# Products that nobody reads, in TensorE's pauses between the sums of a graph attention layer

## The chip, the cores and the metric

The kernel runs on one core of a Trainium2 chip. A core has several engines, each with an instruction stream of its own that it works through in order: TensorE (PE in the profile; its loads of the stationary operand are shown apart, as PEld), VectorE (DVE), ScalarE (ACT), GpSimd (POOL, which here issues the gathers) and SyncE (SP). Engines wait for each other through semaphores; data lie in SBUF, the accumulators of TensorE in PSUM, the inputs and large intermediates in HBM. The metric is the time of one execution in microseconds on the device, less is better.

## The reference

A graph of N = 6250 nodes and E = 100000 edges, width D = 512, H = 8 heads of DK = 64. Edges come sorted by `src`, which is the node that receives. Cut to what matters:

```python
def gnn(x, src, dst, att_bias):                    # x is already normalised
    q, k, v = [(x @ W + b).reshape(n, H, DK) for W, b in ((Wq, bq), (Wk, bk), (Wv, bv))]
    logits = einsum('ehd,ehd->eh', q[src] / sqrt(DK), k[dst]) + att_bias
    p = exp(logits - segment_max(logits, src)[src])
    att = p / segment_sum(p, src)[src]
    y = segment_sum(att[:, :, None] * v[dst], src)
    return y.reshape(n, H * DK) @ Wo + bo

x = x + gnn(layernorm(x), src, dst, edge_attr_8)
x = x + ffn(layernorm(x))
```

The `ffn` is a small network on 160 columns: it decodes two 4-bit numbers per operand and two flags from each row, runs three layers of 160 x 160 with relu between them, and adds a few one-hot values to the row. Everything is float32.

## The kernel before

**Before the main loop (0 to about 640 us).** Keys of the nodes are sorted, so that nodes of like degree are handled together, and TensorE makes k and v for all nodes (L467). They are written to a table in HBM, `kv_d`, with one row of 1024 floats (k, then v) for each node.

**The main loop (about 640 to 3200 us).** The nodes are taken in 49 blocks of 128, one node to a partition. A block has as many slots as its largest degree asks for (`CAP`, 804 slots in all); a slot holds one edge for each of its 128 nodes. A block's slots are split into parts of at most 12, 91 parts in all, and a part is worked on in pairs of slots, 425 pairs in all, each in a buffer `kvt` of shape [128, 2, 1024] from a pool of 11.

For each pair:

- POOL gathers its rows of `kv_d` with one indirect DMA for each slot (L110, `kv<-kv_d,rec`), and somewhat ahead the records of the edges (L110, `rec<-rec_d,eid`).
- `pump()` advances work of other blocks by one step: the next block's projection (`project`: transposes L803, ACT's copy `xT` L805, q from L809 and L810), the end of an earlier part (`part_end`: L1064 and L1068 add its sum p_y to y, L1072 copies a first one), an earlier block's output (`attend_out`: transposes L833 and L834, ACT's copies L836 and L838, the output projection L842 and L843) and steps of the small network (`alu`: L892, L906, L919, L926, L933).
- `dots()`: DVE multiplies the k half by the node's q, in place (L814), and sums by head (L815) into `dot`. After this the k half of the buffer holds products that nothing in the kernel reads again.

At the end of a part, `softmax()` turns `dot` into weights: DVE L744 to L751, ACT's exponential L752, and ACT's copy of the weights into PSUM (L756), into one of the two halves of the tile `pp`, turn by turn. What comes next in a part, `sums()`, is put off until the first pair of the next part has had its `dots()`: the denominator (L767), then for each pair `weigh()` multiplies the v half by the weights, on DVE with the weights read from `pp` (L825), on ACT with a scalar for each head for the last one or two whole pairs (L823), and TensorE adds the slots up into `p_y` by products with the identity matrix (L1105, 1608 passes in all, two for each slot since float32 takes two).

**What sets the order.** The program is written under a manual schedule: each engine does its instructions in the order in which the program issues them. Waits are put in from the tiles that an instruction reads and writes. The tiles of the main loop come from pools with `reuse_waits="tile"`, so a buffer is free again when the last reader of the tile that it held is done. A gather into a `kvt` buffer so waits for the L1105 passes that read it. `pp` is one tile for the whole loop, `tr` has one buffer in PSUM, `q`, `p_y` and `mm` two each.

After the loop the last blocks' outputs and the small network are finished (3200 us to the end).

Of the kernel before, what the change touches and what calls it, by code (L numbers as in the profile page):

```python
# [10 lines left out]
F32 = mybir.dt.float32  # L11
# [9 lines left out]
P = 128  # L21
# [22 lines left out]
def gnn_ffn_kernel(  # L44
# [3 lines left out]
    nc = tc.nc  # L48
    N, D = x.shape
    E = src.shape[0]  # L50
    H = edge_attr.shape[1]
# [22 lines left out]
    def ctile(shape, name, dt=F32, pool=const):  # L74
        return pool.tile(shape, dt, tag=name, name=name)
# [33 lines left out]
    def gather(dst_t, table, idx):  # L109
        nc.gpsimd.indirect_dma_start(  # L110
            out=dst_t, out_offset=None, in_=table,
            in_offset=bass.IndirectOffsetOnAxis(ap=idx, axis=0))
# [4 lines left out]
    wq = ctile([P, KC, D], "wq", pool=ow)  # L117
# [105 lines left out]
    def fetch_keys(b):  # L223
        C = CAP[ORDER[b]]
        t, nbuf = ("0", 1) if b == 0 else ("", LA + 3)
        kg = pre.tile([P, C + 1], F32, tag="kg" + t, name="kg", bufs=nbuf)
        gather(kg, words, pos_i[:, ORDER[b]:ORDER[b] + 1])
        st[b] = dict(kg=kg)

    def read_keys(b):  # L230
        C = CAP[ORDER[b]]
        t, nbuf = ("0", 1) if b == 0 else ("", LA + 3)
        f0 = pre.tile([P, 1], F32, tag="f0", name="f0", bufs=2)
        eid = decode(st[b]["kg"], 1, C, f0, t, nbuf, ids=nid[:, b:b + 1])
        rec = pre.tile([P, C, ROW], F32, tag="rec" + t, name="rec", bufs=min(nbuf, LA + 2))
        st[b].update(rec=rec, eid=eid)
# [10 lines left out]
    def fetch_recs(n, last):  # L247

        while fetched[0] < n and fetched[1] is not None and fetched[1][0] <= last:
            b, s = fetched[1]  # L250
            gather(st[b]["rec"][:, s, :], rec_d, st[b]["eid"][:, s:s + 1])
            fetched[:] = fetched[0] + 1, next(wanted, None)
# [481 lines left out]
    ops = ctx.enter_context(tc.tile_pool(name="ops", bufs=2, space=PSUM, **main))  # L734

    turn_ = [0, 0]
    assert CG * H <= P
    pp = ops.tile([P, 2 * P], F32, tag="pp", name="pp", bufs=1)

    def softmax(lg, rec, m0):  # L740


        n = lg.shape[1]
        nc.vector.scalar_tensor_tensor(lg, lg, SCALE, rec[:, :, 1:], op0=OP.mult, op1=OP.add)  # L744
        m = ap_.tile([P, H], F32, tag="m", name="m", bufs=4)
        nc.vector.tensor_reduce(m, lg.rearrange("p c h -> p h c"), AX.X, OP.max)
        if m0 is None:
            nc.vector.tensor_scalar(m, m, FLOOR, None, op0=OP.max)
        else:
            nc.vector.tensor_tensor(m, m, m0, op=OP.max)  # L750
        nc.vector.tensor_tensor(lg, lg, m[:, None, :].to_broadcast([P, n, H]), op=OP.subtract)  # L751
        nc.scalar.activation(lg, lg, AF.Exp)  # L752
        turn_[1] ^= 1
        p_ps = pp[:, turn_[1] * P:turn_[1] * P + n * H].rearrange(
            "p (c h) -> p c h", h=H)
        nc.scalar.copy(p_ps, lg)  # L756
        cor = None
        if m0 is not None:
            cor = ap_.tile([P, H], F32, tag="cor", name="cor", bufs=3)
            nc.vector.tensor_tensor(cor, m0, m, op=OP.subtract)  # L760
            nc.scalar.activation(cor, cor, AF.Exp)
        return m, cor, p_ps
# [36 lines left out]
    def project(xg, s_):  # L799

        pt = ops.tile([P, KC, P], F32, tag="tr", name="tr", bufs=1)
        for c in range(KC):
            nc.tensor.transpose(pt[:, c, :], xg[:, D + c * P:D + (c + 1) * P], ident)  # L803
        xT = o2.tile([P, KC, P], F32, tag="xT", name="xT", bufs=2)
        nc.scalar.copy(xT, pt)  # L805
        yield
        q = s_["q"] = ops.tile([P, D], F32, tag="q", name="q")
        for c in range(KC):
            nc.tensor.matmul(q, xT[:, c, :], wq[:, c, :], start=(c == 0), stop=False)  # L809
        nc.tensor.matmul(q, ones3, bq3, start=False, stop=True)  # L810

    def dots(kvt, n, q, dot, s):
        k = kvt[:, :n, :D]
        nc.vector.tensor_tensor(k, k, q[:, None, :].to_broadcast([P, n, D]), op=OP.mult)  # L814
        nc.vector.tensor_reduce(  # L815
            dot[:, s:s + n, :], k.rearrange("p s (h d) -> p s h d", h=H), AX.X, OP.add)
# [164 lines left out]
    def fetch_nodes(b):  # L981
        if b - 4 in ends:
            run(ends.pop(b - 4))
        xg = ap_.tile([P, 2 * D], F32, tag="xg", name="xg", bufs=4)
        gather(xg, xx_d, nid[:, b:b + 1])
        st[b]["xg"] = xg
# [17 lines left out]
    def pump(kinds="", n=1):  # L1004

        last[1] += 1
        for g in list(going):
            if next(g, True):
                if g in going:
                    going.remove(g)  # L1010
        alu_steps(kinds, n)
        if stores and stores[0][0] + last[0] <= last[1]:
            store()

    def alu_steps(kinds, n):

        while alus and n > 0 and kind[0] in kinds:
            kind[0] = next(alus[0], None)
            if kind[0] is None:
                alus.pop(0)  # L1020
                kind[0] = "P"
            n -= 1

    def run(g):

        while alus and g in alus and g is not alus[0]:
            run(alus[0])
        for _ in g:
            pass
        if g in alus:  # L1030
            kind[0] = "P"
        for l in (going, alus):
            if g in l:
                l.remove(g)
# [78 lines left out]
    for b in range(NB):  # L1113
        C = CAP[ORDER[b]]
        s_ = st[b]
        rec, q = s_["rec"], s_["q"]
        parts = -(-C // PART)
        m = None
        for i in range(parts):
            s0, s1 = C * i // parts, C * (i + 1) // parts  # L1120
            n_ = s1 - s0
            dot = ap_.tile([P, n_, H], F32, tag="dot", name="dot", bufs=2)
            kvs = []
            for s in range(s0, s1, 2):
                n = min(2, s1 - s)
                kvt = kvp.tile([P, 2, 2 * D], F32, tag="kv", name="kv")
                for j in range(n):
                    gather(kvt[:, j, :], kv_d, rec[:, s + j, 0:1].bitcast(I32))
                kvs.append((kvt, n, s - s0))
                done = sum(SLOTS[:b]) + s + n  # L1130
                if done > HOLD:
                    last[0] = 1000
                fetch_recs(FIRST + (TOTAL - FIRST) * done // (TOTAL - LAST), b + LA)
                if s == s0 and i == 0:
                    if b + LA + 2 < NB:
                        fetch_keys(b + LA + 2)
                    if b + 1 < NB:
                        fetch_nodes(b + 1)
                if s == s0 + 2 and i == 0 and b + 1 < NB:
                    pj = project(st[b + 1]["xg"], st[b + 1])  # L1140
                    going.insert(0, pj)


                k = len(kvs) - 1
                pump("" if k < 2 else "D" if s + 2 >= s1 else "DE" if k == 2 else "DEP")
                dots(kvt, n, q, dot, s - s0)
                if s == s0:
                    for f in waiting:
                        f()
                    waiting.clear()  # L1150
                if s == s0 + 2 and i == parts - 1 and b + LA + 2 < NB:
                    read_keys(b + LA + 2)
            m, cor, p_ps = softmax(dot, rec[:, s0:s1], m)
            waiting.append(partial(sums, b, i, parts, dot, cor, p_ps, kvs, n_))
            alu_steps("P", min(4, len(kvs) - 1))
        if b + 1 < NB:
            run(pj)
# [150 lines left out]
```

## Time and profile before

| what | value |
|---|---|
| median of 14 runs | 3280.02 us |
| lowest and highest run | 3246.71 and 3307.73 us |
| time of the profiled execution | 3278.29 us |
| its span, first to last instruction | 3276.4 us |
| mean granted TensorE clock | 0.799 |
| matmul passes / weight loads on PE | 4853 / 4853 |
| instructions on DVE / ACT / POOL | 3502 / 2656 / 1860 |
| moved by DMA | 542.30 MB, mean 166 GB/s |

In the profile, an instruction's line is that of the kernel printed above. A float32 product appears as two passes, a transpose as one. The row `PEclk` gives the clock that was granted to TensorE in each of 40 slices of the span, in tenths. Three groups of the main loop give the scale: 804 gathers of k and v on POOL, each 946 ns with the next one issued some 0.30 us later; 425 products with q on DVE (L814), which take 1.21 us for a whole pair; 425 sums by head (L815), 1.22 us. The copy of the weights into `pp` (L756, 91 times) has a median of 222 ns. In the tables of waits, "issue" is time in which an engine waited for nothing that the profile shows, and "remote" a wait whose releaser the profile doesn't find among the engines of the core.

### The profile page before, as it was taken

What the parts mean: (1) busy time and instruction counts of PE and PEld (TensorE: products, weight loads), DVE (VectorE), ACT (ScalarE), POOL (GpSimd) and SP (SyncE); (2) the same over time, 40 slices, a digit from 0 to 9 for tenths busy, and PEclk for the clock granted to TensorE, in tenths of its full rate; (3) what the DMA queues carried; (4) which work ended last, traced back from release to release, by engine and by line L of the source; (5) the groups of instructions that cost most, each with busy time, mean ns of one, the idle gap of its engine ahead of it and who ended that gap; (6) DMA issues with size and microseconds to landing.
All of it is one profiled execution on the core that took longest, in us unless ns stands there. A gap on an engine that the chain in (4) does not pass through costs nothing.

```text
span 3276.4 us, 20109 instructions
## 1 busy us (share of the span) xinstructions
PE 2055.4 (63%) x4853; PEld 887.1 (27%) x4853; DVE 2007.9 (61%) x3502; ACT 880.8 (27%) x2656; POOL 1709.0 (52%) x1860
## 2 busy tenths in 40 slices
PE   7887218644545646646566676666756738556686
PEld 3443104211212222222222232222322313222233
DVE  9987000176645657655776767767677657766762
ACT  6443004121212112222132222322313213122333
POOL 2011760274666366555656656666566565656530
PEclk9999659866767867877878787887877878878787
DMA  8543103465445356455656556666566554656530
GB/s 277 176 155 107 20 16 133 143 217 193 162 160 186 116 178 200 158 167 173 205 174 197 182 178 200 197 191 188 171 200 201 161 184 159 207 174 211 170 116 17
DMA packets 193964, 542.30 MB, mean 166 GB/s; under 512 B 51831, under 2 KB 53174, under 8 KB 193841
## 3 DMA queue, kind: packets, MB, share of 16 engines
q0 software_dynamic: 154416, 464.27, 44.5%
q1 hardware_dynamic: 39425, 76.67, 6.7%
q8 instruction: 42, 0.69, 0.1%
q14 instruction: 81, 0.66, 0.1%
HBM read 472.60 MB, written 68.22 MB: 165 GB/s over the span
## 4 chain that ended last, share of the span: by engine, by line
PE 37%; another core or an unknown queue 23%; DVE 18%; issue 12%; ACT 6%; POOL 2%; DMA 1%; POOLq 0%; DVEq 0%; SPq 0%; ACTq 0%
PE p_y L1105 12%; PE pm L467 7%; DVE kv L814 4%; PE q L809 4%; PE pm L919 4%; PE pm L842 3%; ACT kv L823 3%; DVE dot L815 3%; DVE kv L825 3%; PE pm L906 2%; PE p L926 2%; DVE key L143 1%; DVE key L144 1%; DMA kv<-kv_d,rec 1%
## 5 line engine op out<-in xcount | busy, mean ns | idle before, releaser
L110 POOL DMA_INDIRECT kv<-kv_d,rec x804 | 760.2, 946 | 765.7 <-PE p_y L1105 298.9
L1105 PE MATMUL p_y<-kv,ident 128*128 128x512 f32 x1608 | 815.3, 663 | 341.5 <-issue 170.0
L110 POOL DMA_INDIRECT rec<-rec_d,eid x804 | 763.8, 950 | 245.2 <-issue 235.4
L814 DVE TENSOR_TENSOR kv<-kv,q 128x1024 f32<-128x1024 f32 (+1 forms) x425 | 490.6, 1154 | 206.6 <-DMA kv<-kv_d,rec 121.8
L1105 PEld LDWEIGHTS p_y<-kv,ident 128*128 128x128 f32 x1608 | 332.4, 212 | 798.2 <-issue 565.1
L815 DVE TENSOR_REDUCE dot<-kv 128x16 f32<-128x1024 f32 (+1 forms) x425 | 494.0, 1162 | 59.3 <-ACT kv L823 22.6
L809 PE MATMUL q<-wq,xT 128*128 128x512 f32 x392 | 226.0, 730 | 363.8 <-issue 190.6
L823 ACT ACTIVATE kv<-kv,dot 128x64 f32<-128x64 f32 x1568 | 387.9, 336 | 40.1 <-issue 40.1
L825 DVE TENSOR_TENSOR kv<-kv,pp 128x1024 f32<-128x1024 f32 (+1 forms) x327 | 352.9, 1139 | 0.0
L842 PE MATMUL pm<-wo,yT 128*128 128x512 f32 x392 | 213.1, 694 | 178.3 <-ACT yT L836 139.4
L805 ACT COPY xT<-tr 128x512 f32<-128x512 f32 x49 | 28.7, 585 | 703.3 <-remote 409.5
L809 PEld LDWEIGHTS q<-wq,xT 128*128 128x128 f32 x392 | 88.1, 236 | 472.9 <-issue 294.7
L467 PE MATMUL pm<-wv,xnT 128*128 128x512 f32 (+1 forms) x392 | 187.9, 614 | 17.3 <-issue 17.1
L467 PE MATMUL pm<-wk,xnT 128*128 128x512 f32 (+1 forms) x392 | 188.5, 622 | 0.0
L842 PEld LDWEIGHTS pm<-wo,yT 128*128 128x128 f32 x392 | 85.3, 226 | 289.1 <-ACT yT L836 145.3
L1068 DVE TENSOR_TENSOR y<-y,p_y 128x512 f32<-128x512 f32 x42 | 28.7, 684 | 205.8 <-remote 141.0
L767 DVE TENSOR_REDUCE den<-dot 128x8 f32<-128x64 f32 (+6 forms) x91 | 24.8, 273 | 198.9 <-ACT dot L752 127.5
L836 ACT COPY yT<-tr 128x512 f32<-128x512 f32 x49 | 28.6, 584 | 438.9 <-remote 246.6
L478 ACT COPY kvt<-pm 128x512 f32<-128x512 f32 (+1 forms) x98 | 57.1, 583 | 317.8 <-remote 132.3
L416 DVE RECIPROCAL rstd<-rstd 128x7 f32<-128x7 f32 (+4 forms) x9 | 1.7, 186 | 211.3 <-ACT rstd L412 159.1
L110 POOL DMA_INDIRECT xg<-xx_d,nid x49 | 46.2, 942 | 148.0 <-DMA kv_d<-kvt 125.7
L433 PE MATMUL tr<-ident,xn 128*128 128x128 f32 (+1 forms) x196 | 31.7, 289 | 135.0 <-ACT xn L424 93.7
(258 smaller groups left out, 2179.5 us busy)
## 6 DMA issues: line engine op xcount, KB each, us to landing
kv_d<-kvt SPq DMA_DIRECT2D x48, 512.0 KB
rec<-rec_d,eid POOLq DMA_INDIRECT x804
kv<-kv_d,rec POOLq DMA_INDIRECT x804
xt<-in_x_dram SPq DMA_DIRECT2D x48, 256.0 KB
xx_d<-xt SPq DMA_DIRECT2D x48, 256.0 KB
xx_d<-xn SPq DMA_DIRECT2D x48, 256.0 KB
rec_d<-R SPq DMA_DIRECT2D x3, 882.0 KB
bt<-in_edge_attr_dram SPq DMA_DIRECT2D x3, 686.0 KB
```

What stands on the lines that cost most here:

```text
L110: nc.gpsimd.indirect_dma_start(out=dst_t, out_offset=None, in_=table, in_offset=bass.IndirectOffsetOnAxis(ap=idx, axis=0))
L467: nc.tensor.matmul(pm[:r], xnT[b][:, c, :r], wkv[nm_][:, c, :], start=(c == 0), stop=(i == 1 and c == KC - 1))
L809: nc.tensor.matmul(q, xT[:, c, :], wq[:, c, :], start=(c == 0), stop=False)
L814: nc.vector.tensor_tensor(k, k, q[:, None, :].to_broadcast([P, n, D]), op=OP.mult)
L815: nc.vector.tensor_reduce(dot[:, s:s + n, :], k.rearrange("p s (h d) -> p s h d", h=H), AX.X, OP.add)
L823: nc.scalar.mul(v[:, i, h], v[:, i, h], p[:, s + i, h:h + 1])
L825: nc.vector.tensor_tensor(v, v, p_ps[:, s:s + n, :, None].to_broadcast([P, n, H, DK]), op=OP.mult)
L842: nc.tensor.matmul(pm, yT[:, c, :], wo[:, c, :], start=(c == 0), stop=False)
L906: nc.tensor.matmul(pm[:, :nt], w0[:, c * P:(c + 1) * P], fT[:, t0:t1], start=True, stop=True)
L919: nc.tensor.matmul(pm[:, :nt], w, h1[:, k, :nt], start=(i == 0), stop=(i == len(terms) - 1))
L926: nc.tensor.matmul(p3[:, :nt], w2[:, c, :], h2[:, c, :nt], start=(c == 0), stop=(c == NC4))
L1105: nc.tensor.matmul(p_y, ident, kvt[:, j, D:], start=(done_ == 0), stop=(done_ == n_ - 1))
```

## The change

The tile `pp` is made twice as wide, and its new half becomes the target of products that nobody reads. In each part, for each pair but the first, after the pair's `dots()` TensorE gets two such products. Each loads 16 columns of the previous pair's k half (after DVE's product with q, hence "one pair behind") as the stationary operand, streams 256 columns of one 128-row block of the query weights `wq`, and writes a [16, 256] result into the new half of `pp`. Nothing else is changed.

```diff
@@ -735,7 +735,8 @@
     turn_ = [0, 0]
     assert CG * H <= P
-    pp = ops.tile([P, 2 * P], F32, tag="pp", name="pp", bufs=1)
+    pp = ops.tile([P, 4 * P], F32, tag="pp", name="pp", bufs=1)
+    idle = pp[:2 * H, 2 * P:]
@@ -1144,6 +1145,12 @@
                 k = len(kvs) - 1
                 pump("" if k < 2 else "D" if s + 2 >= s1 else "DE" if k == 2 else "DEP")
                 dots(kvt, n, q, dot, s - s0)
+
+                if s > s0:
+                    for c in range(2):
+                        nc.tensor.matmul(
+                            idle, kvs[-2][0][:, 0, :2 * H],
+                            wq[:, c, :2 * P], start=True, stop=True)
                 if s == s0:
                     for f in waiting:
                         f()
```

Here `s0` is the first slot of the part, `s` the first slot of the pair, and `kvs` the list of the part's pairs so far, so that `kvs[-2][0]` is the previous pair's buffer.

## The prediction

> **What bounds the kernel now.** I read the page's head first, for the engines and the granted clock, and then the chain that ended last.
>
> ```profile
> PE 2055.4 (63%) x4853; PEld 887.1 (27%) x4853; DVE 2007.9 (61%) x3502; ACT 880.8 (27%) x2656; POOL 1709.0 (52%) x1860
> ...
> PEclk9999659866767867877878787887877878878787
> ...
> PE 37%; another core or an unknown queue 23%; DVE 18%; issue 12%; ACT 6%; POOL 2%; DMA 1%; POOLq 0%; DVEq 0%; SPq 0%; ACTq 0%
> ```
>
> No engine is full. TensorE (PE) carries the largest share of the chain, at a clock granted at 0.6 to 0.8 of full speed through the main loop (640 to 3200 us). There is one core, so "another core" needs an explanation, and the table of waits gives it.
>
> ```profile
> ACT xT L805 <- remote: 409.5, 15, 46.6
> POOL kv L110 <- PE p_y L1105: 298.9, 60, 30.7
> ACT yT L836 <- remote: 246.6, 14, 41.6
> ```
>
> The "remote" waits (us in total, times, longest) are ACT copies of transposes that PE's records show finished long before. PE's signals come late, up to 46.6 us, in 29 episodes on these two lines, 656 us together; the profile does not say why. I call them holds. PE and these waits for PE make 37 + 23 = 60% of the chain. The second row is POOL out of gather buffers, because PE has not summed the old ones. The timeline of one part then shows the place that the change touches, just after such a hold.
>
> ```profile
> 2426.10 0.58 ACT L805 COPY xT<-tr 128x512 f32<-128x512 f32 x1 [33.78 <-remote]
> ...
> 2426.74 5.16 PE L809 MATMUL q<-wq,xT 128*128 128x512 f32 x8 [22.09 <-ACT xT L805]
> 2426.86 0.21 ACT L756 COPY pp<-dot 128x56 f32<-128x56 f32 x1
> ...
> 2427.10 2.95 DVE L825 TENSOR_TENSOR kv<-kv,pp 128x1024 f32<-128x1024 f32 x3
> ...
> 2431.73 0.38 PE L810 MATMUL q<-bq,ones 65*128 65x512 bf16 x1
> ...
> 2431.95 6.17 PE L1105 MATMUL p_y<-kv,ident 128*128 128x512 f32 x14
> ```
>
> Each row has its start and its time. The weights go into the tile pp at 2426.86 while PE still makes q; DVE weighs three pairs under that; PE sums at 2431.95 without a pause. That overlap is what is at stake.
>
> **The change, part by part.** *Products.* 425 pairs in 91 parts give 425 - 91 = 334 places with two products, 668 in all, each of two passes as every f32 matmul here: 1336 passes of 256 columns. Their price comes from rows of that width:
>
> ```profile
> 3218.20 2.33 PE L926 MATMUL p<-h,w 128*8 128x256 f32 x10
> ```
>
> Ten passes take 2.33 us, so one starts every 0.22 us at clock 1.0 (less 0.16 us of tail), twice that at 0.5: 0.86 us a pair warm, 1.71 cold, 288 us or 572 us in all. PE is idle 2560 - 1581 = 979 us of the loop (windows view), so they fit in time that is free on average.
>
> *A wait that the diff does not spell out.* The scratch target is a slice of pp itself, and hazards are kept by tile. In the built programs all 91 copies L756, which waited for ACT alone, now also wait for PE to finish the last products of their own part, and 42 of DVE's L825 do too. PE works in program order, so these products stand behind whatever the pump put ahead of them: q (L809, L810), the output projection (L842, L843), the small network (L892, L906). Behind the waiting copy on ACT stand L761, the weighing on ACT (L823) and the next xT or yT copy; behind L825 stand DVE's dots for the next pairs; behind those p_y, and then POOL, whose buffers p_y frees. POOL's own waits and its queue, SP and the DMAs are unchanged in number.
>
> In the part shown, q ends at 2431.73 + 0.38 = 2432.11. Two pairs of products follow it, 2 x 0.86 = 1.7 us, so the copy starts at 2433.8 instead of 2426.86: 7.0 us late. DVE's next rows were back to back in that stretch, so it loses the 7.0 us. PE's sums start after copy and first weighing, 2433.8 + 0.2 + 1.2 = 2435.2 instead of 2431.95.
>
> I did this for each part: the recorded end of the last PE row ahead of the part's last products, and the end of DVE's product that they load, the later of both plus the warm price of the products there (2.05 pairs on average after the last useful row), against the start of that part's copy. 64 of the 91 copies come late, by 296 us together, 4.6 us each; at the cold price 73 copies, 443 us. In 50 parts the useful row alone ends after the copy (27 times q, 17 the output projection, 6 L892).
>
> What of 296 us reaches the end? The lower end is nothing, if every late copy falls into slack; the upper is 443 us, cold and all on the chain. DVE is busy 1704 of 2560 us of the loop (67%), and 60% of the chain hangs on PE or its signals. I take 60%: 296 x 0.6 = +178 us.
>
> *The clock.* I cut the loop into windows of 3.413 us, aligned to the steps of the granted clock. Of 69 windows at 1.0 in which PE was busy less than 0.4, all 69 were followed by one at 0.5; of 11 between 0.4 and 0.5, 8 stayed. From 0.5, none of 222 windows less than 0.8 busy was followed by one at 1.0. One pair of the first kind:
>
> ```profile
> 2317.08:2320.49 3.41, 1.21 (x5) 0.60 (x5) 3.17 (x8) 0.00 (x0) 2.79 (x3) 1.00 0.94 316
> 2320.49:2323.90 3.41, 0.96 (x6) 0.51 (x3) 0.71 (x1) 0.00 (x0) 2.50 (x4) 0.50 0.67 208
> ```
>
> The first figures after the length are PE's busy us; 1.00 and 0.50 are the granted clocks: 1.21 us busy (0.35) did not hold it. Products give (0.86 + 0.16) per pair. Where DVE sets the pace (L814 1.21 + L815 1.22 = 2.43 us) that is 0.42, on the edge; where POOL does (four gathers of 0.95 + 0.30 = 5.0 us) it is 0.20, and lost. Cold, 1.71 + 0.16 in 2.43 us is 0.77, still short of raising it. So the pauses mostly stay cold, and the gain is that bursts start warm in some parts. Rows of PE that start at 0.5 fill 467 us of the loop, so they cost 234 us more than at 1.0: this is the ceiling; the floor is 0, or a loss if products that run cold ahead of a burst delay it, which the 443 us hold. I take a quarter, -58 us, since only DVE-paced pauses that began warm keep the clock.
>
> The Trainium skill weighs this otherwise: its page "TensorE: Matmul & The Clock Gate", section "HAM oscillation — how this bites in real kernels", puts the drop down to idle gaps in PE's work that outlast some 3.4 us. By it the products of DVE-paced pauses would hold 1.0 surely and the gain would be nearer the ceiling, about 3220 us with the wait counted; the trace, where 0.35 busy lost the clock, decides here.
>
> *pp twice as wide* and the slice cost no instruction: 0.
>
> Sum against the profiled execution, 3276.4 of span and 1.9 around it: 3278.3 + 178 - 58 = 3398, and as that execution lay 1.7 us under the median, 3400 us, +3.7%. Its own range takes 40% of the late copies with half the clock's ceiling (+118 - 117, about 3280) as too kind and so starts at 3310, and ends with 80% of them and no gain (+237, 3517).
>
> **The rivals.** *It keeps PE warm, and is faster.* Place: pauses paced by DVE. If 1.0 holds through them, the whole 234 us x 0.6 = -140 goes, and q and the output projection, now warm, end earlier, so that perhaps half of the late copies remain (+89): 3229, say 3225 us. It decides where windows in pauses reach 0.4 busy, thus at pair periods up to 2.5 us. For it: at 0.42 the products are just over the edge. Against it: POOL fetches a pair in 5.0 us, the loop takes 2560 / 425 = 6.0 us a pair, and only 430 of 749 windows are at 1.0 to begin with. Chance 0.13.
>
> *It hides.* POOL's gathers set the pace, (1608 + 147) x 1.25 = 2194 us of the loop's 2560, and late copies only use up PE's and DVE's slack: 3280, chance 0.10. Against it: POOL stands 298.9 us waiting for p_y, which late copies lengthen.
>
> *The holds grow.* They start only while gathers run back to back at clock 1.0, and passes complete in them some 2.8 us apart whatever their size. The loop spends 656 of 2560 us in them, so 1336 x 0.26 = 342 passes would fall into holds; at 2.8 us that is up to 960 us, of which POOL running out of buffers, which ends a hold, should leave a quarter: +240 on top of the 120, 3640 us, and from 3517 up this case decides. For it: more passes for the same signals. Against: a hold's end comes from POOL, not from PE. Chance 0.20.
>
> **How the numbers follow.** Likeliest (products and wait on the chain) 0.57, faster 0.13, no change 0.10, holds 0.20. A measurement of this kernel tells about 0.5%, 16 us, from no change; so faster 0.13, same 0.10, slower 0.77. The range leaves out some 0.1 at each end: from 3265, which keeps the upper edge of the faster case, to 3610, inside the case of the holds.
>
> **What would show it.** In the profile after: 1336 passes of the new line, near 0.43 us spacing where they run alone; ACT's pp copy with idle time released by PE, some 60 times and 5 us each; DVE's L825 or den rows with new waits; POOL's wait for p_y longer than 298.9 us; the clock near 0.80, not 0.9. A mean clock over 0.88 with the pp copy waiting under 150 us would make the forecast wrong on the fast side; "remote" waits well over 656 us on the slow side.

## The result, and the profile after

The changed kernel takes 3539.68 us (median of 10 runs, 3510.19 to 3559.47) against 3281.28 us (47 runs of the kernel before). The ratio is 1.0823, with a 95% interval from 1.0788 to 1.0859: 8.2% slower, 258 us. The forecast had +3.7% (3400 us). The profiled execution takes 3537.49 us, its span is 3535.7.

The head of the page of the changed kernel: engines' busy times, the granted clock by slices, the chain that ended last.

```profile
PE 2396.0 (68%) x6189; PEld 1000.7 (28%) x6189; DVE 2010.6 (57%) x3502; ACT 878.1 (25%) x2656; POOL 1707.8 (48%) x1860
...
PEclk9998569778788777788797788878878879879897
...
PE 37%; another core or an unknown queue 25%; DVE 19%; issue 13%; ACT 4%; POOL 1%; DMA 1%; ACTq 0%; POOLq 0%; DVEq 0%; SPq 0%
```

The passes went from 4853 to 6189, the 1336 that were counted. The mean granted clock went from 0.799 to 0.817 only. DVE, ACT and POOL have the same busy us as before, spread over a longer span. From the first copy into pp to the last it took 2526.7 us before (661.2 to 3187.9) and takes 2780.9 us now (664.9 to 3445.8), so 254 us of the difference lie in the main loop, spread over its whole length.

The groups of instructions of the changed kernel: busy us and mean ns, then the engine's idle us just ahead of them and what ended most of it. The new line of the products is L1151; other lines stand one higher than before.

```profile
L110 POOL DMA_INDIRECT kv<-kv_d,rec x804 | 759.1, 944 | 1014.7 <-PE p_y L1106 392.8
L1106 PE MATMUL p_y<-kv,ident 128*128 128x512 f32 x1608 | 824.4, 671 | 362.7 <-DVE kv L826 240.2
...
L826 DVE TENSOR_TENSOR kv<-kv,pp 128x1024 f32<-128x1024 f32 (+1 forms) x327 | 353.1, 1140 | 199.8 <-ACT pp L757 132.5
...
L1151 PE MATMUL pp<-wq,kv 128*16 128x256 f32 x1336 | 335.9, 390 | 24.3 <-DVE kv L815 15.3
...
L757 ACT COPY pp<-dot 128x64 f32<-128x64 f32 (+6 forms) x91 | 20.2, 222 | 592.4 <-remote 344.7
```

Two rows of the same groups before:

```profile
L110 POOL DMA_INDIRECT kv<-kv_d,rec x804 | 760.2, 946 | 765.7 <-PE p_y L1105 298.9
...
L825 DVE TENSOR_TENSOR kv<-kv,pp 128x1024 f32<-128x1024 f32 (+1 forms) x327 | 352.9, 1139 | 0.0
```

POOL's idle time ahead of the gathers grew from 765.7 to 1014.7 us, by 249 us. That is nearly the whole loss, as it has to be for an engine whose busy time stayed the same. The other rows show the path that the forecast named, with the new wait at its start. ACT stands idle for 592.4 us ahead of the copy into pp; DVE's weighing, which never waited, now waits 199.8 us; PE's sums wait 240.2 us for DVE's weighing (94.7 before); then buffers come free later and POOL waits. What the copy waits for, in us and times:

```profile
  remote: 344.7, 43
  PE pp L1151: 118.2, 19
  issue: 62.4, 9
  PE pm L920: 33.9, 4
  PE pm L907: 21.9, 2
  PE p L927: 10.9, 1
```

The larger part is not PE's rows but "remote": the product has ended in the records and the copy still does not start. The timeline shows one such wait (start, us, engine and line):

```profile
1484.37 2.76 PE L1151 MATMUL pp<-wq,kv 128*16 128x256 f32 x12
...
1487.07 0.66 PE L834 MATMUL tr<-ident,y 128*128 128x128 f32 x4
1487.11 0.95 POOL L110 DMA_INDIRECT rec<-rec_d,eid  x1 [0.30 <-issue]
1487.56 0.27 PE L835 MATMUL p_y<-ident,some 128*66 128x128 f32 x1
...
1499.61 0.94 POOL L110 DMA_INDIRECT xg<-xx_d,nid  x1 [0.30 <-issue]
1504.66 0.23 ACT L757 COPY pp<-dot 128x80 f32<-128x80 f32 x1 [20.96 <-remote]
...
1504.92 1.22 DVE L826 TENSOR_TENSOR kv<-kv,pp 128x1024 f32<-128x1024 f32 x1 [18.87 <-ACT pp L757]
```

The next rows of PE and of POOL, each from the timeline of its engine alone, show how the wait is handed on:

```profile
1506.20 11.30 PE L1106 MATMUL p_y<-kv,ident 128*128 128x512 f32 x20 [18.36 <-DVE kv L826]
```

```profile
1510.25 0.94 POOL L110 DMA_INDIRECT kv<-kv_d,rec  x1 [9.70 <-PE p_y L1106]
```

The last products end at 1484.37 + 2.76 = 1487.13 and the copy starts at 1504.66, 17.5 us later; DVE stands still for 18.87 us, PE's sums for 18.36. POOL goes on issuing gathers until 1500.55, runs out of buffers and waits 9.70 us for the sums; the copy gets its signal 4.1 us after the last gather. The same stretch in windows (first figures: length, PE's busy us and rows; then PEld, DVE, ACT, POOL; the last three are granted clock, DMA share, GB/s):

```profile
1487.30:1491.00 3.70, 0.53 (x5) 0.27 (x3) 0.00 (x0) 0.00 (x0) 2.78 (x4) 0.96 0.66 237
1491.00:1494.00 3.00, 0.00 (x0) 0.00 (x0) 0.00 (x0) 0.00 (x0) 2.39 (x3) 0.50 0.82 239
...
1501.00:1504.60 3.60, 0.00 (x0) 0.00 (x0) 0.00 (x0) 0.00 (x0) 0.00 (x0) 0.50 0.46 146
```

The clock fell to 0.50 in the middle of the wait, as it does when PE is idle. The trace also holds the times at which PE's semaphore was raised. The last product and the last rows of L834 and L835 end at 1487.14, 1487.72 and 1487.83 in the records; their three signals come together at 1504.58, 1504.64 and 1504.67. So the records seem to be right, PE has nothing to do, and what comes late is the signal that it is done.

I split the wait ahead of each copy at the recorded end of the last product ahead of it. Up to that end: 259 us in 53 copies. After it: 319 us in 56 copies.

### The profile page after: what moved, and what is told of

The parts are those of the page before. It is cut to its first block, busy times and chain, and to the rows that moved or that the text cites. A ratio compares the mean times of both kernels' runs of the same rounds, so it can differ in the third digit from the quotient of the medians.

```text
span 3535.7 us, 22758 instructions
## 1 busy us (share of the span) xinstructions
PE 2396.0 (68%) x6189; PEld 1000.7 (28%) x6189; DVE 2010.6 (57%) x3502; ACT 878.1 (25%) x2656; POOL 1707.8 (48%) x1860
## 4 chain that ended last, share of the span: by engine, by line
PE 37%; another core or an unknown queue 25%; DVE 19%; issue 13%; ACT 4%; POOL 1%; DMA 1%; ACTq 0%; POOLq 0%; DVEq 0%; SPq 0%
PE p_y L1106 13%; PE pm L467 7%; PE pm L920 5%; DVE kv L815 5%; DVE dot L816 3%; PE pm L843 3%; DVE kv L826 3%; PE pp L1151 2%; PE pm L907 2%; PE q L810 2%; ACT kv L824 2%; DVE key L143 1%; DVE key L144 1%; PE p L927 1%
## 5 line engine op out<-in xcount | busy, mean ns | idle before, releaser
L110 POOL DMA_INDIRECT kv<-kv_d,rec x804 | 759.1, 944 | 1014.7 <-PE p_y L1106 392.8
L1106 PE MATMUL p_y<-kv,ident 128*128 128x512 f32 x1608 | 824.4, 671 | 362.7 <-DVE kv L826 240.2
L826 DVE TENSOR_TENSOR kv<-kv,pp 128x1024 f32<-128x1024 f32 (+1 forms) x327 | 353.1, 1140 | 199.8 <-ACT pp L757 132.5
L1151 PE MATMUL pp<-wq,kv 128*16 128x256 f32 x1336 | 335.9, 390 | 24.3 <-DVE kv L815 15.3
L810 PE MATMUL q<-wq,xT 128*128 128x512 f32 x392 | 193.1, 638 | 79.2 <-issue 71.8
L1151 PEld LDWEIGHTS pp<-wq,kv 128*16 128x16 f32 x1336 | 113.5, 97 | 230.2 <-issue 92.4
L907 PE MATMUL pm<-fT,w 8*128 8x512 f32 (+2 forms) x140 | 104.0, 870 | 102.0 <-ACT h L909 49.0
L757 ACT COPY pp<-dot 128x64 f32<-128x64 f32 (+6 forms) x91 | 20.2, 222 | 592.4 <-remote 344.7
L810 PEld LDWEIGHTS q<-wq,xT 128*128 128x128 f32 x392 | 75.0, 201 | 178.4 <-issue 163.5
```

What stands on the lines that cost most here:

```text
L110: nc.gpsimd.indirect_dma_start(out=dst_t, out_offset=None, in_=table, in_offset=bass.IndirectOffsetOnAxis(ap=idx, axis=0))
L826: nc.vector.tensor_tensor(v, v, p_ps[:, s:s + n, :, None].to_broadcast([P, n, H, DK]), op=OP.mult)
L907: nc.tensor.matmul(pm[:, :nt], w0[:, c * P:(c + 1) * P], fT[:, t0:t1], start=True, stop=True)
L1106: nc.tensor.matmul(p_y, ident, kvt[:, j, D:], start=(done_ == 0), stop=(done_ == n_ - 1))
L1151: nc.tensor.matmul(idle, kvs[-2][0][:, 0, :2 * H], wq[:, c, :2 * P], start=True, stop=True)
```

## The experiments

**The chips are not alike.** The first four runs fell on one chip, where the kernel before takes 3285 us; the runs of the forecast and of the result (3281 us, with the same late signals) are counted with it, though the record names no chip for them. All later ones fell on three other chips, where it takes 2638 to 2640 us. I call them chip A and chips B. Each run is compared with the kernel before on its own chip. In the profile of before, "remote" ends idle time of engines 117 times, 1231 us together; in none of the 14 profiles taken on chips B does it appear at all.

| kernel | chip A | chips B |
|---|---|---|
| before | 3284.63 us | 2638 to 2640 us |
| as changed | 1.0823 [1.0788, 1.0859] (the result) | 1.0175 [1.0158, 1.0192] |
| thin products, wait kept | 1.0703 [1.062, 1.0786] | 1.0021 [1.0012, 1.0031] |
| one thin product a part, wait kept | not run | 1.0004, 1.0015, 1.0010, 1.0016 |
| products early in the part | 1.0829 [1.0763, 1.0895] | not run |
| weights in SBUF, no products (base) | 0.9989 [0.9947, 1.0031] | 1.0437 [1.042, 1.0455] |
| weights in SBUF, thin products | not run | 1.0427, 1.0445, 1.0435, 1.0431 |
| weights in SBUF, full products | 1.0324 [1.0255, 1.0393] | 1.0462 [1.0445, 1.048] |
| weights in SBUF, four products a pair | not run | 1.0526 [1.0505, 1.0547] |

The first two theories were the late copy (the wait makes the price) and PE's work (the products' own time makes it).

**Thin products (e1).** The wait stays, the products shrink from 256 columns to 2.

```diff
-                            idle, kvs[-2][0][:, 0, :2 * H],
-                            wq[:, c, :2 * P], start=True, stop=True)
+                            idle[:, :2], kvs[-2][0][:, 0, :2 * H],
+                            wq[:, c, :2], start=True, stop=True)
```

> The products stay where they are, with the same waits, but stream 2 columns of wq instead of 256 (the result is 16 x 2), so that they cost PE almost nothing. The changed kernel takes 258 us more than before (3540 against 3281). Theory of the late copy: the time comes from the copy of the weights into pp, which now waits for PE (idle time before it on ACT 530 us, ended by PE or by 'remote'); the products' own length hardly counts, so thin products keep most of it: +5 to +8% (3445 to 3540 us), and the copy still waits over 350 us. Theory of PE's work: the 336 us of products standing ahead of useful rows are the cost, so thin ones are within 1.5% of before. If both share, in between, and the product's length is worth the rest.

Measured on chip A: +7.0%, 3521 us. Most of the loss, 7.0 of 8.2%, stays with products that are next to nothing. The waits ahead of the copy in this run:

```profile
  remote: 463.8, 52
  PE pp L1151: 84.0, 15
```

By the same split, 176 us lie before the recorded end of the products and 448 us after it. So on this chip it is not the length that hurts most, and late signals make most of the copy's wait.

**Products early in the part (e2).** All products, full length, moved to the second pair.

```diff
-                if s > s0:
-                    for c in range(2):
+                if s == s0 + 2:
+                    for c in range(2 * len(range(s0 + 2, s1, 2))):
                         nc.tensor.matmul(
                             idle, kvs[-2][0][:, 0, :2 * H],
-                            wq[:, c, :2 * P], start=True, stop=True)
+                            wq[:, c % KC, :2 * P], start=True, stop=True)
```

> All 668 products, at full length, but those of a part are all issued at its second pair (stationary: the first pair's product), so that the pump's later steps (q, output projection, small network) no longer stand ahead of the part's last product. Late copy: the wait of the copy is over long before the softmax in most parts, so the kernel falls back to before plus 0 to 3% (3280 to 3380 us) and the copy's waits for PE drop under 150 us. PE's work: same passes, so still +6 to +9%.

Measured on chip A: +8.3%, a miss for the theory of the late copy. The copy's "remote" wait fell to 229.5 us, and the recorded ends account for only 58 us of its waits. But other waits grew:

```profile
POOL kv L110 <- PE p_y L1106: 529.8, 82, 26.3
...
ACT pp L757 <- remote: 229.5, 30, 33.1
...
ACT yT L837 <- remote: 188.3, 10, 36.6
ACT xT L806 <- remote: 176.9, 6, 49.5
```

(Us in total, times, longest.) "remote" ended 1492 us of idle time in all here, against 1242 in the changed kernel. Early products still stand behind the sums of the part before in PE's order, so the copy still cannot run ahead of those sums, and q, the output projection and the small network stand behind the whole bunch. Which of these keeps the time up was not separated. What the run does show is that the us of the copy's wait are not the price one for one.

**Nobody waits for the products (e3, e4).** DVE takes the weights from SBUF and nothing is copied into pp; e3 does this to the kernel before, e4 to the changed one. The copy L756 is left out.

```diff
-        nc.scalar.copy(p_ps, lg)
...
-                v, v, p_ps[:, s:s + n, :, None].to_broadcast([P, n, H, DK]), op=OP.mult)
+                v, v, p[:, s:s + n, :, None].to_broadcast([P, n, H, DK]), op=OP.mult)
```

> The kernel before, without the change, with DVE weighing from the weights in SBUF and no copy into pp: the base for the next run. 91 copies of 0.22 us go from ACT's chain; whether DVE's weighing (1.14 us a pair) gets slower with both operands in SBUF is unknown. Both theories: within 2% of before, unless the weighing's time changes.

> As the run before it, with the change's products: pp now has no other writer or reader, so neither ACT nor DVE waits for the products. Late copy: against the base without products 0 to +2.5% (PE's in-order delay alone), or a little faster if the clock stays up. PE's work: against that base still +6 to +9%.

(The weighing still writes into a buffer that the products read, but in e4's trace no weighing, on DVE or on ACT, waits for PE's semaphore.) Measured on chip A: the base is as fast as before (3286 us), and with the full products it takes 3392 us: 3391.52 / 3285.86 = 1.032, 106 us. Without the wait, more than half of the loss is gone: 258 - 106 = 152 us go with it. The rest is more than the late copy's theory allowed and less than that of PE's work. The run with products:

```profile
PE 2382.7 (70%) x6189; PEld 997.6 (29%) x6189; DVE 2005.6 (59%) x3502; ACT 858.9 (25%) x2565; POOL 1791.0 (53%) x1860
...
L110 POOL DMA_INDIRECT kv<-kv_d,rec x804 | 797.2, 992 | 772.8 <-PE p_y L1105 364.3
...
L1150 PE MATMUL pp<-wq,kv 128*16 128x256 f32 x1336 | 341.8, 394 | 27.2 <-issue 15.5
...
L825 DVE TENSOR_TENSOR kv<-kv,dot 128x1024 f32<-128x1024 f32 (+1 forms) x327 | 354.2, 1143 | 0.0
```

and its base:

```profile
PE 2046.8 (63%) x4853; PEld 886.1 (27%) x4853; DVE 2007.2 (61%) x3502; ACT 863.8 (26%) x2565; POOL 1795.1 (55%) x1860
...
L110 POOL DMA_INDIRECT kv<-kv_d,rec x804 | 800.2, 995 | 661.8 <-PE p_y L1104 224.5
```

DVE no longer waits ahead of its weighing (0.0). POOL's idle time ahead of the gathers grows by 111 us, and its wait for the sums, the largest part of it, from 224.5 to 364.3. And PE's other work got no faster: 2382.7 - 341.8 = 2040.9 us against 2046.8. The products bought 6 us of PE's time for 342 us of their own.

**On chips B (e5 to e7, e9 to e18).** These runs were meant for the rest of the column of chip A. e5 to e7 were the thin products with the weights in SBUF, four products a pair (`range(4)`), and the wait with one thin product in each part (`if s > s0 and s + 2 >= s1:`, `range(1)`).

> Weights read from SBUF, so that nobody waits for the products, and the products stream 2 columns instead of 256. Against the same kernel with full products (3392 us, 3.2% over its base of 3286): theory of length: what is left without the copy's wait is PE's time in its order, so thin products fall back to the base, 3270 to 3305 us. Theory of signals: what is left comes from more passes and signals on PE, whose delivery is late while POOL issues gathers, so thin products keep most of it, 3350 to 3400 us, with 'remote' waits as in the run with full products.

> As the kernel with weights from SBUF and products, but four products a pair instead of two (1336 products, some 576 us of PE at the full clock). Theory of length: PE's pauses are used up, the cost more than doubles, +7 to +10% over the base of 3286 (3510 to 3615 us). Theory of signals: it grows by less than half, +3 to +5%. If the products keep the clock at 1.0 the mean granted clock goes to over 0.88 and part comes back; at two a pair it was 0.824 against 0.801.

> The wait alone: in place of two products for each pair, a single product of 2 columns at the last pair of each part (91 products, 182 passes of about 0.06 us), written into pp as in the change, so that the copy of the weights waits for PE as it does there. Theory of the late copy: the wait is the cost, so the kernel stays at +5 to +7% (3445 to 3515 us) like the thin products (+7.0%). If the number of products counts: under +2%.

The base for e5 and e6 was not known on these chips; e12, below, gives it: reading the weights from SBUF costs 4.4% here. e5 is then the base (1.0427), and e6 with 1336 products is 2776.3 / 2752.66 = 0.9% slower than e5, beside it on the same chip. e7 is within 0.04% of before. Neither theory had this; the next runs were made to see what the change itself does here.

> The changed kernel itself. The kernel before took 3281 to 3285 us in the runs that forecast and first experiments rest on, with late signals of PE ('remote' waits); on the chip of the last four runs it took 2638 us and showed no such waits. If this run falls on a chip like the first: +8% again, 3520 to 3560 us. If on one like the second: theory that the late signals make the price of the wait: +2 to +5% (products' own time and some late copies on a loop that POOL's gathers pace), clearly under +8%. Rival, that the wait costs alike everywhere: +7 to +9%.

> One product of 2 columns a part, with the change's wait: the same kernel as the run that was within 0.1% of before on a chip without late signals. On a chip like that again 0 to +0.3%. On a chip with late signals: if the wait alone is the price, +5 to +7%; if the number of products (their passes and signals) makes it, under +2%.

> Products of 2 columns that nobody waits for, weights read from SBUF; base is the next run. On a chip with late signals: theory of length 0 to +0.7% over the base; theory of signals +2 to +4%. On a chip without: within 0.5% of the base.

> The kernel before with weights read from SBUF, the base. On a chip with late signals within 0.5% of before, as measured (0.999). On a chip where POOL's gathers pace the loop: slower by 3 to 5%, because a gather's issue takes 0.995 us there instead of 0.946 while DVE works from SBUF alone (1755 gathers in the loop, 0.05 us each, 86 us), which would also explain most of the +4.3% of the thin products measured there.

The change as it is costs 1.75% on chips B, about a fifth of what it costs on chip A: far from the +7 to +9% of the rival, and a little under the +2 to +5% expected for a chip without late signals. The page of that run, and what ended its waits of two kinds:

```profile
PE 2275.9 (85%) x6189; PEld 962.8 (36%) x6189; DVE 2006.9 (75%) x3502; ACT 879.6 (33%) x2656; POOL 1708.4 (64%) x1860
...
PEclk9999999688888889889998999998999989998997
```

```profile
ACT pp L757 <- PE pp L1151: 203.1, 57, 6.0
...
DVE kv L826 <- ACT pp L757: 54.8, 23, 5.1
...
POOL kv L110 <- PE p_y L1106: 47.2, 57, 8.2
```

Here the copy waits for PE's rows alone: 197 us in 53 copies up to the recorded end of the products, next to nothing after it. That is near the 259 us of chip A; the 319 us of late signals are what is missing. DVE feels 54.8 us of it, and the kernel loses 1.75% of 2637.53, 46 us. The mean granted clock rose to 0.915, against 0.871 with one thin product a part, whose row of busy times is

```profile
PE 2019.8 (76%) x5035; PEld 880.2 (33%) x5035; DVE 2008.2 (76%) x3502; ACT 879.1 (33%) x2656; POOL 1708.0 (65%) x1860
```

There PE's other work did get shorter, 2275.9 - 335.0 = 1940.9 us against 2019.8 - 18.6 = 2001.2 (the groups of the products have 335.0 and 18.6 us busy), 60 us, and the kernel got nothing from it. Without the wait it is the same: 2289.6 - 338.9 = 1950.7 us in e16 against 2021.3 in e12, and no gain in time. With four products a pair (e6) the mean clock is 0.948 against 0.855 in e12 and PE's other work 2507.6 - 621.4 = 1886.2 us, 135 us less, and the kernel is 0.9% slower than e12. e12's expectation held: 1.0437, with a gather's issue at 1016 ns in its groups.

That POOL sets the pace on chips B can be read from the window of e10's main loop, beside that of before on chip A (POOL's are the last busy us and count ahead of the clock):

```profile
490.00:2545.00 2055.00, 1543.51 (x3654) 647.61 (x3655) 1693.19 (x2683) 643.57 (x2156) 1525.74 (x1609) 0.86 0.71 225
```

```profile
640.00:3200.00 2560.00, 1580.78 (x3485) 658.22 (x3483) 1703.74 (x2719) 653.31 (x2180) 1521.54 (x1603) 0.79 0.56 180
```

At 1.25 us from one issue to the next, 1609 instructions of POOL need some 2010 us of the 2055 on chips B, and 1603 need some 2000 us of the 2560 on chip A.

> One product of 2 columns a part with the change's wait. Chip with late signals (before near 3280): wait alone, +5 to +7%; number of products, under +2%. Chip without (before near 2638): 0 to +0.3%, as twice before.

> Products of 2 columns that nobody waits for. Chip with late signals: base there 3286 (0.999 of before); theory of length -0.3 to +0.8% of before; theory of signals +2 to +4%. Chip without: +4.4% of before, like its base.

> Products of 2 columns for every pair, with the change's wait. Chip with late signals: +7.0% again. Chip without: the full products cost +1.75% there and a single thin one a part +0.1%; if the length of the products makes the 1.75%, 0 to +0.4%; if their place in PE's order and the number of waits make it, +1 to +1.75%.

> Full products that nobody waits for, weights from SBUF. Chip with late signals: +3.2% again. Chip without: its base is +4.4% of before there, four products a pair were +5.3%; so two +4.4 to +5.0%, 0 to 0.6% over the base.

> One product of 2 columns a part with the change's wait, once more for a chip with late signals (before near 3280): wait alone, +5 to +7%; number of products, under +2%. On a chip without (before near 2638): 0 to +0.3%, as on three chips so far.

> Products of 2 columns that nobody waits for. Chip with late signals: if the length of the products made the +3.2% of the full ones there, -0.3 to +0.8% of before; if their passes and signals made it, +2 to +4%. Chip without: +4.3 to +4.5%, like its base.

All six fell on chips B and repeat or complete their column. Thin products with the wait: +0.2%. Full products without it: 2760.60 / 2752.61 = +0.3% over thin ones on the same chip. Both together, as changed: +1.75%. So on chips B neither the wait nor the length costs much alone; what costs is a full product that somebody waits for. One reservation: the runs without the wait have slower gathers (1016 ns in e12 against 944 in e10), so they may hide products that would show at the faster pace; this was not separated. The row of waits agrees: DVE waits 22.2 us for the copy with thin products and 54.8 us with full ones, 33 us of the 41 us by which 1.0175 and 1.0021 differ.

**A break for POOL (e8).** In the kernel before, a POOL instruction that does nothing useful after each pair's gathers.

```diff
+    gap_ = ap_.tile([P, 256], F32, tag="gap", name="gap", bufs=1)
...
                 kvs.append((kvt, n, s - s0))
+                nc.gpsimd.memset(gap_, 0.0)
```

> The kernel before, without the change, with one POOL memset of 128 x 256 after the gathers of each pair, 425 in all, which nobody reads. In the trace of before, PE's signals that come late arrive only some 3.4 us after POOL has stopped issuing gathers (POOL quiet from 1842.2, signals at 1845.55 to 1845.64), while the granted clock falls as if PE were idle. Theory: gathers issued back to back hold PE's signals up, so short breaks let them through: the 'remote' waits of xT and yT (656 us) fall by over a third, and the time is within -4 to +2% of before. Rival: the holds have nothing to do with POOL's issue: 'remote' waits unchanged, the time up by 0 to 4%.

It fell on a chip B, where there are no late signals to mend, so it says nothing of the theory. It took 1.0277 of before [1.0256, 1.0298], 73 us, where POOL's busy time is 1854.4 us against some 1708 us with the same gathers in the kernels above: on chips B a delay of POOL goes into the time by half.

## Why the prediction was right or wrong

**Right:** the direction; the count of 1336 passes and their price at the full clock, one every 0.22 us (0.38 us for a pass on its own, 2.76 us for twelve; 1289 of the 1336 start while the granted clock is 1.0); the wait that the diff does not spell out, its place (the copy into pp, then DVE's weighing, the sums, POOL's buffers) and its number (some 60 copies; 69 waited for PE or a late signal by the profile's list, 57 on chips B); and that the mean clock would hardly move on that chip (0.817).

**The late copies, forecast 296 us of which 178 reach the end.** The arithmetic took the recorded ends of PE's rows. For that it was near: 259 us on chip A, 197 on chips B. But the copy waits for the signal, not for the record, and 319 us more came from signals that were late. The forecast had these holds before its eyes, 656 us of them on two lines, and put them into a rival in which more passes make them longer, instead of asking who else would now wait in them. The share that reaches the end, 60%, was too high in turn: taking the wait away gives 152 us (e4) and the wait with thin products costs 231 us (e1, 0.0703 x 3284.63), while the copies are late by 259 + 319 = 578 and 176 + 448 = 624 us: 26 to 37%. Two errors in opposite directions left a term, 178 us, that lies between the two measurements: that it came near is luck. The "late, up to 46.6 us" of the forecast was a misreading too: 46.6 us is the whole idle time of ACT ahead of that copy, and the recorded end lies 33.8 us before it:

```profile
1166.40 0.60 PE L803 MATMUL tr<-ident,xg 128*128 128x128 f32 x4
...
1200.17 0.95 POOL L110 DMA_INDIRECT rec<-rec_d,eid  x1 [0.30 <-issue]
1200.76 0.59 ACT L805 COPY xT<-tr 128x512 f32<-128x512 f32 x1 [46.64 <-remote]
```

**The clock, forecast -58 us: this is the step that failed.** It stood for all that the products do besides the wait, and it was a gain. Without the wait the products cost 106 us on chip A (e4 against e3); on top of thin ones with the wait, 1.0823 - 1.0703 is 39 us, with an uncertainty of about 30. PE's other rows did not get shorter: 2396.0 - 335.9 = 2060.1 us against 2055.4 before. Those of q did (L809, now L810: 226.0 to 193.1 us), those of the small network got longer (L906, now L907: 89.5 to 104.0). The rows that start at the clock of 0.5, which the forecast put at 467 us of the loop and counted on to become fewer, fill 485 us now without the products, against 461 before by the same count. The forecast had shown that 0.35 of a window does not hold the clock and put the products at 0.42 at best, and still booked a quarter of the ceiling. And it priced the passes themselves at nothing because PE is idle 979 us of the loop, without asking what is queued behind them on PE: q, the projections, the sums. That this queue makes the 106 us is the likeliest reading (POOL's wait for the sums grew by 140 us in e4), but no run shows it.

The split depends on the order in which the two are taken away. With the wait taken first it is 152 and 106 us, which make up 258 by construction; with the products made thin first it is 231 for the wait and 39, give or take 30, for their length. Either way the term that stood at -58 is a cost, and where the forecast had 178 - 58 = 120 us, 258 were measured.

**The rivals.** *Keeping PE warm* failed twice: on chip A the clock did not rise enough, and on chips B it rose to 0.915 and shortened PE's other work by 60 us without shortening the kernel. *Hidden* is near the truth on chips B for products that nobody waits for (+0.3%). Its sum was too high for chip A: (1608 + 147) x 1.25 counts all of POOL's gathers, while the window of the loop above has 1603 instructions, some 2000 us instead of 2194, so POOL was further from setting the pace there than the forecast had it. *The holds grow* named 3517 us as the point from which it decides, and 3540 lies above it; late signals do decide, but not as it said. They did not get longer in total: "remote" ends 1242 us of idle time now and 1231 before. Their place changed: xT's 409.5 us went down to 117.1, and the copy, which had no part in them, took 344.7. Nor does POOL have to run out of buffers for a hold to end, as the forecast had it: in the rows of before shown above, a gather starts 0.6 us ahead of the copy.

**Left open.** On chip A, whether the wait alone, with a single product a part, makes the 7% (e7 and its repeats fell on chips B), whether it is the length or the number of the products that makes the 106 us (e5 and its repeats likewise), what kept e2 slow, why that chip's signals come late, and whether it is the chip itself, which was met in one group of runs only, or something else about that group.

## What to carry to other kernels

A product that nobody reads still has a place to write to: if that place shares a tile with something on the chain, the filler becomes a dependence, and the price is set by when its completion is seen, which need not be when its rows end: with late signals thin products kept 7.0 of the 8.2%, without them thin ones cost 0.2% and full ones 1.75%. Before filling an engine's pauses, list who waits on that engine in its order, and take the lateness of its signals from the waits in the trace rather than from the recorded ends of its rows. And a faster clock on an engine is worth what the kernel's pace leaves of it: 60 us less work of PE, and 135 in e6, bought nothing where POOL's gathers set the pace.

## What the runs showed of the hardware

- The same kernel took 3285 us on one chip and 2638 us on three others, with the runs of before in one group together within 62 us (chip A, 3262.70 to 3324.70) and within 12 us (chips B). On the slower chip PE's signals arrive up to 42.0 us after the recorded end: in the changed kernel the transposes below end at 1167.10 and the copy that waits for them starts at 1209.11. In the example at 1487 us the clock fell to 0.5 meanwhile. In 9 of the 20 longest waits of the copy in the changed kernel the signal came 3.8 to 5.1 us after the last gather began, as in the example above, and in the other 11 within 2.8 us of one. That POOL's issue holds the signals up is thus not shown.

```profile
1166.50 0.60 PE L804 MATMUL tr<-ident,xg 128*128 128x128 f32 x4
...
1209.11 0.58 ACT L806 COPY xT<-tr 128x512 f32<-128x512 f32 x1 [54.43 <-remote]
```

- The clock kept to the same bounds on both kinds of chip. In six profiles (before, as changed on both chips, e4, e6, e10), from 660 us on to 200 us before the end, all 281 windows of 3.413 us at 1.0 with PE busy under 0.4 were followed by one at 0.5, and of 58 between 0.4 and 0.5, 27 stayed at 1.0; of 703 windows at 0.5 with PE busy under 0.8, none was followed by one at 1.0. The Trainium skill ("TensorE: Matmul & The Clock Gate", section "HAM oscillation — how this bites in real kernels") asks for no idle gaps of PE above some 3.4 us, the length of such a window; here a window that was partly busy lost the clock too.
- DVE's weighing slows POOL's issue when both of its operands lie in SBUF: 995 ns for a gather of k and v in e3 against 946 ns before on chip A, 1016 in e12 against 944 in e10 on chips B. The 175 of POOL's gathers in e3 that overlap a weighing take 1441 ns on average and the others 950; before, with the weights in PSUM, 946 and 950. It costs nothing where POOL waits for buffers anyway (0.9989) and 4.4% where POOL sets the pace.
- The Trainium skill ("PSUM — Partial Sum Buffer", section "PSUM bank collisions raise a hardware error") says that an engine must not touch a bank and quadrant that TensorE is writing. In this program the waits come from the tile that the products share with the weights; no run here tried the overlap without the wait.
